# Four GNN layers on one core: norms scaled by ScalarE alone, part of VectorE's work given to GpSimd, kept blocks copied first, and a new order

## The chip, the cores and the metric

The kernel runs on one core of one Trainium2 chip. The metric is the device time of one execution, in microseconds (us). Every run below was in the fast state, and each was timed in turns with the kernel before on the same chip.

## The reference, cut to what matters

Sixteen graphs (batches) of 1024 nodes with 128 features go through four layers. All is fp32. Each layer adds its result to `x`.

```python
def layer(x, gnn):                       # 4 times
    h = jnp.maximum(_layernorm(x), 0.0)
    return x + gnn(h, adj, ...)

# layer 0, three times: a square of the nodes, weighted by the adjacency
h = h @ W + b
nh = h / jnp.maximum(jnp.linalg.norm(h, axis=-1, keepdims=True), EPS)
ew = adj * jnp.einsum('bij,bkj->bik', nh, nh)
h = jnp.einsum('bpq,bqc->bpc', ew, h)

# layer 1: (1 + eps) * x + adj^T x, then an MLP (128 -> 256 -> 128)

# layer 2: attention of tanh(s1 + s2); nodes without neighbours keep h ("lone nodes")
return jnp.where(su == 0, node_embedding, last_h)

# layer 3: gated attention over a symmetric square
att = jax.nn.softmax(jnp.where(adj > 0, e, 0), axis=1) * adj
h_prime = jax.nn.relu(jnp.einsum('bij,bjk->bik', att, h))
i_c, f_c, o_c = sigmoid(...), sigmoid(...), sigmoid(...)      # one per node
return o_c * jnp.tanh(jax.nn.sigmoid(i_c * h_prime + f_c * x))
```

## The kernel before

The kernel first writes down all its operations with an estimated duration, what they read and what they write. A planner then orders them in a simulated time: of the operations that an engine could begin now it takes the one with the smallest rank. The rank is the deadline of the batch, less the longest chain behind the operation, less a hand-set lead for its kind. The program is emitted in that order, so **each engine works through a fixed sequence**, and an operation whose input is late holds up all behind it on its engine.

```python
for o in reversed(self.ops):
    o.tail = o.us + max((s.tail + o.lat for s in o.succs), default=0.0)
    o.rank = (self.deadline(o.batch) - o.tail - self.leads.get(o.key, 0.0), o.seq)
```

Layer norms: VectorE scales four of the eight blocks, ScalarE the other four (and applies relu to its own; a separate ScalarE relu follows for VectorE's, except in layer 0):

```python
dve(1.03, [blk(xt, lo, hi), mv, rstd], [blk(hn, lo, hi)], lambda: scale_by_vector(*HALVES[0]), True)
lo, hi = HALVES[1]
act(1.55, [blk(xt, lo, hi), nb, rstd], [blk(hn, lo, hi)], lambda: scale_by_scalar(*HALVES[1]))
```

A symmetric square is computed by rows of blocks, half a row (512 columns, one PSUM bank) at a time. Blocks right of the diagonal are kept in SBUF (`above`), and the rows below turn them instead of computing them. A VectorE multiply reads each half row out of PSUM, and then ScalarE copies the kept blocks of the same bank:

```python
pc, view = square.row(j, s)                       # TensorE: matmul and turned blocks
dve(..., nc.vector.scalar_tensor_tensor(ew, view(), rn, adjT, op0=mult, op1=mult))
square.keep(j, s, pc)                             # ScalarE: copy of the kept blocks
```

Layer 3's rows, and its finish:

```python
# each row j: mask (VectorE), row maximum (VectorE), exp with sum (ScalarE), then
for lo, hi in HALVES:
    nc.vector.tensor_mul(span(e.t, lo, hi), span(e.t, lo, hi), span(aT[j].t, lo, hi))
# ... finish of a batch
nc.gpsimd.tensor_mul(z, hn, gate_f)               # GpSimd
add_scaled(z, D, 0, NB, hp, 0, E3, gate, 0, z, True)          # VectorE, 8 instructions
act(..., squash)                                  # two tanh
add_scaled(z, D, 0, NB, z, 0, D, gate, 2 * NB, xt, True)      # VectorE, 8 instructions
```

## Time and profile before

| | before |
|---|---|
| median (3 runs) | 2484.54 us (2484.53 to 2487.31) |
| span of the profiled run | 2481.8 us |
| what TensorE's rows need back to back (worked out in the prediction, which rounds it to 2371) | 2371.6 us |
| the rest | 110.2 us |

The rest can be placed in time. For a given TensorE row, sum the durations of all rows ahead of it in TensorE's order, and subtract the sum from the time at which the row really ran. I call the difference the **surplus**; what it grows by over a stretch is what TensorE lost there. I read it at each batch's first `psN` (the last projection of layer 3).

The waits of TensorE in the kernel before (columns: what waited for what, us in total, times, longest):

```profile
PE sq L619 <- ACT above L641: 27.8, 18, 2.0
PE ps_hT L451 <- DVE hn L553: 10.3, 1, 10.3
PE acc L671 <- DVE ew L791: 4.5, 3, 3.0
```

The first row is the copy of kept blocks, about once a batch; the second is the start of the program, which waits for the first norm.

### The profile page before, as it was taken

The numbers are of one execution on the slowest core, as the hardware profiler recorded it, in microseconds if no ns is written. First come the engines' busy times: TensorE is split into PE (matmuls) and PEld (weight loads), VectorE is DVE, ScalarE is ACT, GpSimd is POOL, SyncE is SP. The second block draws the span as 40 slices with busy tenths as digits, with TensorE's granted clock in tenths as the row PEclk, the third lists the DMA queues.
The fourth block names the chain that finished last, engine by engine and source line by source line (L and its number), as shares of the span: only waits on it lengthen the run. The fifth ranks groups of instructions, "written<-read, shape, count | busy, mean of one in ns | idle before, by whom it ended". The sixth has DMA issues, their size and how long they took to land.

```text
span 2481.8 us, 34726 instructions
## 1 busy us (share of the span) xinstructions
PE 2410.6 (97%) x11946; PEld 1588.7 (64%) x11946; DVE 2119.4 (85%) x5278; ACT 1287.1 (52%) x2401; POOL 214.4 (9%) x134
## 2 busy tenths in 40 slices
PE   6999999999999999999999999999999999999987
PEld 3567566675766657566675766756566575765763
DVE  6767989898897989889898897988989899796777
ACT  4425554644646455454554636456454655554575
POOL 1000010010101011011010100101011010010100
PEclk9999999999999999999999999999999999999998
DMA  7622827648284563936648276473945638054100
GB/s 125 129 67 69 163 59 143 138 80 167 60 160 121 99 140 84 165 91 127 129 94 178 52 154 135 84 154 68 165 107 111 136 85 162 1 108 80 35 1 18
DMA packets 1129441, 263.35 MB, mean 106 GB/s; under 512 B 971824, under 2 KB 1112880, under 8 KB 1129264
## 3 DMA queue, kind: packets, MB, share of 16 engines
q1 hardware_dynamic: 1108352, 251.73, 50.0%
q10 hardware_dynamic: 20912, 9.40, 1.4%
q8 instruction: 94, 1.54, 0.3%
q14 instruction: 83, 0.68, 0.1%
HBM read 198.14 MB, written 62.91 MB: 105 GB/s over the span
## 4 chain that ended last, share of the span: by engine, by line
PE 78%; DVE 9%; ACT 7%; issue 2%; DMA 1%; SPq 1%; ACTq 0%; POOL 0%; POOLq 0%; DVEq 0%
PE acc L671 31%; PE sq L609 17%; PE acc L682 11%; PE psP L461 6%; PE sq L619 4%; ACT e L906 3%; DVE ew L791 3%; ACT e L910 3%; PE py L844 2%; PE py L471 2%; DVE e L914 2%; PE ps_hTn L451 1%; DVE z L505 1%; PE pg L471 1%; PE ps_hnT L451 1%
## 5 line engine op out<-in xcount | busy, mean ns | idle before, releaser
L791 DVE SCALAR_TENSOR_TENSOR ew<-sq,rn,adjT 128x512 f32<-128x512 f32 x612 | 436.9, 739 | 68.2 <-PE sq L619 32.0
L671 PE MATMUL acc<-ew,h 128*128 128x512 f32 x1024 | 480.6, 597 | 4.7 <-DVE ew L791 4.5
L609 PE MATMUL sq<-hTn 128*128 128x512 f32 (+3 forms) x1152 | 441.3, 489 | 0.4 <-ACT hTn L483 0.4
L641 ACT COPY above<-sq 128x384 f32<-128x384 f32 (+3 forms) x432 | 169.2, 394 | 403.9 <-DVE ew L791 366.5
L671 PEld LDWEIGHTS acc<-ew,h 128*128 128x128 f32 x1024 | 178.9, 191 | 174.0 <-issue 112.9
L609 PEld LDWEIGHTS sq<-hTn 128*128 128x128 f32 x1152 | 193.5, 191 | 124.0 <-issue 76.1
L682 PEld LDWEIGHTS acc<-h,e 128*128 128x128 f32 x2048 | 241.0, 192 | 29.3 <-DVE e L914 11.8
L682 PEld LDWEIGHTS acc<-h,ew 128*128 128x128 f32 x2048 | 240.8, 192 | 21.0 <-DVE ew L791 11.4
L444 POOL TENSOR_TENSOR rstd<-ve,mhalf 128x8 f32<-128x8 f32 x64 | 104.8, 1637 | 1725.7 <-DVE ve L536 1694.9
L682 PE MATMUL acc<-h,ew 128*128 128x128 f32 x2048 | 252.7, 276 | 0.4 <-DVE ew L791 0.4
L682 PE MATMUL acc<-h,e 128*128 128x129 f32 x2048 | 249.5, 277 | 2.8 <-DVE e L914 1.5
L671 PE MATMUL acc<-e,hs 128*128 128x512 f32 x512 | 240.6, 595 | 1.7 <-DVE e L995 1.7
L671 PE MATMUL acc<-adjL,hn 128*128 128x512 f32 x512 | 239.0, 595 | 0.1
L988 ACT ACTIVATE e<-e,top 128x1024 f32<-128x1024 f32 x128 | 147.1, 1149 | 173.0 <-DVE top L984 172.5
L735 ACT ACTIVATE adjT<-adjT 128x1024 f32<-128x1024 f32 x128 | 135.0, 1055 | 194.0 <-DVE adjT L732 163.7
L619 PEld LDWEIGHTS sq<-ident,above 128*128 128x128 f32 x960 | 125.7, 141 | 142.2 <-issue 74.0
L619 PE MATMUL sq<-ident,above 128*128 128x128 f32 x960 | 174.4, 275 | 27.8 <-ACT above L641 27.8
L914 DVE SCALAR_TENSOR_TENSOR e<-adjT,e 128x512 f32<-128x512 f32 x256 | 162.0, 683 | 41.9 <-ACT e L910 41.9
L732 DVE STREAM_TRANSPOSE adjT<-adjT 128x1024 f32<-128x1024 f32 x128 | 155.2, 1225 | 17.8 <-DMA adjT<-in_adj_dram 10.9
L995 DVE TENSOR_TENSOR e<-e,adjT 128x512 f32<-128x512 f32 x256 | 166.2, 680 | 0.0
L906 ACT ACTIVATE e<-s,h 128x1024 f32<-128x1024 f32 x128 | 143.1, 1141 | 38.4 <-issue 36.6
L631 DVE STREAM_TRANSPOSE above<-sq 128x512 f32<-128x512 f32 x208 | 147.0, 707 | 10.5 <-PE sq L609 9.1
(124 smaller groups left out, 3455.9 us busy)
## 6 DMA issues: line engine op xcount, KB each, us to landing
adjT<-in_adj_dram SPq DMA_DIRECT2D x512, 128.0 KB, 3.7
adjL<-in_adj_dram SPq DMA_DIRECT2D x128, 512.0 KB, 4.9
by_hbm<-above SPq DMA_DIRECT2D x104, 512.0 KB, 3.2
got<-by_hbm SPq DMA_DIRECT2D x416, 128.0 KB, 3.0
x<-in_x_dram SPq DMA_DIRECT2D x16, 512.0 KB, 5.3
out_dram<-z ACTq DMA_DIRECT2D x16, 512.0 KB, 3.3
b<-in_L_gnn_b_dram ACTq DMA_DIRECT2D x4, 64.0 KB, 3.8
w<-in_L_gnn_W_dram ACTq DMA_DIRECT2D x2, 128.0 KB, 3.8
```

What stands on the lines that cost most here:

```text
L461: nc.tensor.matmul(dst.t[:, (c - lo) * n : (c - lo + 1) * n], cols(srcT.t, c), w, start=True, stop=True)
L609: lambda: nc.tensor.matmul(dst.t[:, (first - lo) * P :], cols(leftT.t, j), span(rightT.t, first, hi), start=True, stop=True),
L619: nc.tensor.transpose(cols(dst.t, r), cols(above.t, p), ident)
L641: lambda: nc.scalar.copy(span(above.t, p, p + hi - first), read.t[:, (first - lo) * P :]),
L671: lambda s=s, lo=lo, hi=hi: nc.tensor.matmul(acc[s].t, cols(h.t, at, w), span(ew.t, lo, hi), start=(j == 0), stop=(j == NB - 1)),
L682: nc.tensor.matmul(a.t[:, (c - lo) * n : (c - lo + 1) * n], cols(ew.t, c), h.t[:, j * w : j * w + n], start=(j == 0 and c == lo), stop=(j ...
L732: dve(V(N), [t], [t], lambda t=t: nc.vector.transpose(t.t, t.t), True)
L791: lambda view=view, ew=ew, rn=rn, j=j, lo=lo, hi=hi: nc.vector.scalar_tensor_tensor(by_block(span(ew.t, lo, hi), D, 4), view(), rn.t[:, j ...
L906: lambda e=e, j=j: nc.scalar.activation(e.t[:, 0:N], s1.t[:, 0:N], AF.Tanh, bias=h.t[:, j * E2 + D + 1 : j * E2 + D + 2]),
L914: lambda e=e, j=j, lo=lo, hi=hi: nc.vector.scalar_tensor_tensor(span(e.t, lo, hi), span(aT[j].t, lo, hi), 0.0, span(e.t, lo, hi), op0=ALU. ...
L988: lambda e=e, top=top, tot=tot: nc.scalar.activation(e.t[:, 0:N], e.t[:, 0:N], AF.Exp, bias=top.t, accum_out=tot.t),
L995: lambda e=e, j=j, lo=lo, hi=hi: nc.vector.tensor_mul(span(e.t, lo, hi), span(e.t, lo, hi), span(aT[j].t, lo, hi)),
```

## The change

The intent: VectorE is at 85%, and where it is late, TensorE stands. So take work off VectorE: norms wholly to ScalarE, layer 3's odd rows, layer 2's lone nodes and layer 3's two last scalings to GpSimd. Let the copy of kept blocks go ahead of VectorE's multiply of the same bank. Plan anew, with leads of their own for the first two and last two batches. The diff, cut to its core:

```diff
+            lead = self.leads.get(o.key + o.edge, self.leads.get(o.key, 0.0))
+            o.rank = (self.deadline(o.batch) - o.tail - lead, o.seq)
 ...
-    PERIOD, LAST, AHEAD, WINDOW = 66.0, 23.0, 2, 0.05
+    PERIOD, LAST, AHEAD, WINDOW = 83.0, 1.0, 2, 0.02
 ... (other buffer limits, all leads new; estimates +0.03 us on ScalarE, +0.015 on VectorE)
+    def on_pool(a, w, scalar, of_node, b, dst):
+        v = lambda: by_block(a.t, w)[:, :, 0:D]
+        pool_op(1.9, [a, scalar], [a], lambda: nc.gpsimd.tensor_mul(v(), v(), per_node(of_node())))
+        pool_op(1.9, [a, b], [dst], lambda: nc.gpsimd.tensor_add(by_block(dst.t), v(), by_block(b.t)))
 ... layer norm: both halves by ScalarE, with relu; no separate relu
+            for lo, hi in HALVES:
+                act(1.55, [blk(xt, lo, hi), nb, rstd], [blk(hn, lo, hi)], lambda lo=lo, hi=hi: scale_by_scalar(lo, hi))
 ... layers 0 and 3: the copy is declared ahead of the multiply
                     pc, view = square.row(j, s)
+                    if "k" in FLAGS:
+                        square.keep(j, s, pc)
                     o = dve(
 ...
-                    square.keep(j, s, pc)
 ... layer 2
-        add_scaled(xt, D, 0, NB, hn, 0, D, alone, 0, xt, True)
+            on_pool(hn, D, alone, lambda: alone.t, xt, xt)
 ... layer 3, rows 1, 3, 5, 7
+                pool_op(1.96, [e, aT[j]], [e], lambda e=e, j=j: nc.gpsimd.tensor_mul(e.t[:, 0:N], e.t[:, 0:N], aT[j].t))
 ... finish of layer 3 (the last batch in two halves): each of the two scalings
+                    pool_op(us, ..., lambda: nc.gpsimd.tensor_mul(part(a, w), part(a, w), per_node(of(g), n)))
+                    pool_op(us, ..., lambda: nc.gpsimd.tensor_add(part(z), part(a, w), part(c)))
 ... batch 0's input is loaded in two halves
```

## The prediction

> **What bounds the kernel now.** I read the page's first two parts, then the engine busy times over chosen stretches of time, then the waits and the timeline around the one wait that recurs, then the groups by form for the cost of what is moved.
>
> The page of the kernel before, busy time and forty slices:
>
> ```profile
> PE 2410.6 (97%) x11946; PEld 1588.7 (64%) x11946; DVE 2119.4 (85%) x5278; ACT 1287.1 (52%) x2401; POOL 214.4 (9%) x134
> ...
> PE   6999999999999999999999999999999999999987
> ...
> PEclk9999999999999999999999999999999999999998
> ```
>
> TensorE is full from the second slice to the last but one. So the question is how much of the span TensorE needs whatever the others do. The instruction orders of both kernels hold the same 3737 TensorE rows, differently ordered. From back-to-back pieces of the chain (a matmul stands there as two records): 512 columns take 0.859 us (8.59 us for 10, batch 0's layer 1), 128 columns 0.2234 (3.57 for 16, L844), 129 to 131 columns 0.227 (7.26 for 32, layer 2), a transpose 0.1097 (an estimate from the step between one and four in a row). 1504 x 0.859 + 128 x 0.644 + 128 x 0.43 + 1809 x 0.2234 + 1408 x 0.227 + 1988 x 0.1097 = **2371 us of TensorE demand**. The span is 2481.8, so all that any reordering can win is in the other **110 us**.
>
> Where these lie: I set the summed demand of all rows ahead of a batch's first psN (layer 3's last projection) against the time at which it runs. The surplus is 17.4 us at the first square (23.6 us), 31.8 at 80.5 us, 39.6 at batch 0's psN (307.7 us), then grows by 3.1 per batch to 74.6 at batch 11 (1959.9 us), is 78.2 at batch 13 (2274.9), 91.6 at batch 14 (2450.9), and 110 at the end. So **head 40, middle 35, tail 35**. Busy times over stretches (columns: stretch, its length, busy of TensorE, its weight loads, VectorE, ScalarE, GpSimd, then clock):
>
> ```profile
> 0.00:50.00 50.00, 32.77 (x124) 19.89 (x125) 28.06 (x74) 22.01 (x43) 7.29 (x10) 0.92 0.80 125
> 1209.86:1359.87 150.01, 148.22 (x735) 97.60 (x734) 133.64 (x333) 78.77 (x147) 13.35 (x9) 1.00 0.58 121
> 2125.10:2274.90 149.80, 149.62 (x759) 99.50 (x758) 121.51 (x291) 82.07 (x149) 11.72 (x7) 1.00 0.39 78
> 2274.90:2450.90 176.00, 168.47 (x915) 117.82 (x914) 139.88 (x373) 103.62 (x187) 13.36 (x8) 0.97 0.04 13
> 2450.90:2482.00 31.10, 13.07 (x60) 7.81 (x58) 19.07 (x54) 12.94 (x25) 3.79 (x2) 0.78 0.13 34
> ```
>
> The second row is one middle batch: demand 146.9 in 150.0 us, VectorE at 133.6 (89%). The third has VectorE at 121.5 (81%), and there demand (149.2) nearly fills the time: lighter VectorE, almost no loss. In the middle TensorE stands still only once a batch, and this is where:
>
> ```profile
> 1254.79 0.81 PE L609 MATMUL sq<-hTn 128*128 128x384 f32 x2
> ...
> 1255.99 0.74 DVE L791 SCALAR_TENSOR_TENSOR ew<-sq,rn,adjT 128x512 f32<-128x512 f32 x1
> ...
> 1256.77 0.48 ACT L641 COPY above<-sq 128x384 f32<-128x384 f32 x1 [6.14 <-DVE ew L791]
> ...
> 1257.30 0.33 PE L619 MATMUL sq<-ident,above 128*128 128x128 f32 x1 [1.70 <-ACT above L641]
> ```
>
> The square is finished at 1255.6, VectorE comes to it 0.4 us late, ScalarE (idle for 6.14 us) may copy the block only after that, and TensorE waits 1.70 us for the copy.
>
> **What the Trainium skill says.** "Perfetto Trace Analysis", Identifying the Most-Contended Engine: matmul busy time is a poor measure of the distance to the roofline, as matmuls are pipelined. The trace agrees: 2410.6 busy against 2371 of demand, so some 39 us of "busy" is stretched. "PSUM — Partial Sum Buffer", PSUM bank collisions raise a hardware error: two engines must not be in the same bank at once, so VectorE's multiply and ScalarE's copy of one square must follow each other; the trace shows the copies waiting for L791 for 366.5 us in 164 waits. "GPSIMD Engine Reference", Engine selection: elementwise work with two inputs is about twice as slow there as on VectorE. Here 1.90 us for 128x1024 against 2 x 0.68. "SBUF — State Buffer", Who interferes with whom: a VectorE instruction with two SBUF inputs and a GpSimd instruction that reads SBUF exclude each other. The kernel before has too little GpSimd work (9%) to show it.
>
> **The change part by part.** Costs by group and form (busy, mean ns of one; in a run of small ones they overlap):
>
> ```profile
> L995 DVE TENSOR_TENSOR e<-e,adjT 128x512 f32<-128x512 f32 x256 | 166.2, 680 | 0.0
> ...
> L560 ACT ACTIVATE hn<-x,nb,rstd 128x128 f32<-128x128 f32 x256 | 105.2, 484 | 26.1 <-DVE nb L544 25.0 <-DVE sum L1000 1.0
> ...
> L553 DVE TENSOR_SCALAR hn<-x,mv,rstd 128x128 f32<-128x128 f32 x256 | 70.4, 337 | 6.9 <-POOL rstd L444 6.9
> ...
> L505 DVE SCALAR_TENSOR_TENSOR x<-hn,alone,x 128x128 f32<-128x128 f32 x128 | 36.6, 357 | 1.3 <-ACT hn L575 1.3
> ...
> L1043 POOL TENSOR_TENSOR z<-hn,gate 128x1024 f32<-128x1024 f32 x16 | 30.4, 1897 | 73.0 <-PE sq L619 40.6 <-DVE gate L1038 21.4 <-PE p L895 11.0
> ```
>
> - Layer norms by ScalarE alone: VectorE loses 256 instructions, 70.4 us. ScalarE gains as many, +105.2, and loses 48 separate relus (30.4): +75.
> - Layer 3's odd rows on GpSimd: VectorE loses 128 of 256 L995, 83 us. GpSimd gains 64 x 1.9 = 122.
> - Layer 2's lone nodes and both last scalings on GpSimd: VectorE loses 3 x 128 small ones (36.6 + 34.5 + 34.5 = 106). GpSimd gains two instructions for each group, 6 per batch x 16 x 1.9 = 182.
> - Sum: VectorE 2119 - 259 = **1860 (75%)**, some 117 per middle batch; ScalarE about **1362 (55%)**; GpSimd about 214 + 304 = **518 (21%)**. No engine overtakes TensorE, and none of the 259 us is on its path: they only remove lateness.
> - Copy first: in the stop shown, the copy could begin at 1255.7 instead of 1256.77. With the lighter VectorE I expect the loss of 3.1 per middle batch to fall to about 1.5: 11.5 x 1.6 = **-18 us**.
> - Head: batch 0's input comes in halves, but its first norm is now ScalarE's alone, 8 x 0.41 = 3.3 us in place of 1.1 beside 1.6. These cancel. Loads of adj (all in the same order) set the rest. The own leads put batch 0 ahead of batch 1: **-4**.
> - Tail: in the new order all of batch 14 is done before batch 15's layer 3, whose last 31.6 us of demand now run alone; before, batch 14's last rows were mixed in. From its first transposes to the end the kernel before took 65.7 us (2416.1 to 2481.8). Now: some 9 us to the first square (12.7 before, 2416.1 to 2428.8, with 3.1 of batch 14's work between); VectorE's 8 rows, 16 x 0.66 + 8 x 1.21 + 8 x 0.65 + 8 x 0.15 = 26.7 (31.9 before), about 28 with waits; then from the last multiply to the end, 20.8 before. The finish goes from one pass of 8.9 us (1.9 + 2.2 + 2.2 + 2.2 and hops, below) to two halves with 10 GpSimd steps of about 1.05 in a row, 10.5 plus hops: +2. Sum about 59. Ahead of it, where 13 us were lost between batches 13 and 14, I expect 4 less.
>
> ```profile
> 2468.78 1.90 POOL L1043 TENSOR_TENSOR z<-hn,gate 128x1024 f32<-128x1024 f32 x1 [11.36 <-DVE gate L1038]
> 2470.71 2.19 DVE L505 SCALAR_TENSOR_TENSOR z<-hp,gate,z 128x128 f32<-128x128 f32 x8 [2.07 <-POOL z L1043]
> ...
> 2475.26 2.19 DVE L505 SCALAR_TENSOR_TENSOR z<-z,gate,x 128x128 f32<-128x128 f32 x8 [2.36 <-ACT z L1050]
> 2477.52 0.38 ACTq L1056 DMA_DIRECT2D out_dram<-z  x1
> ```
>
> Sum: at batch 15's first layer-3 transpose the demand done is 2340.0 in the new order. The surplus there was 87.1; less 18, 4 and 4 it is 61. 2340 + 61 + 59 = 2460 of span; timed runs lie 2.7 above the span (2484.5 against 2481.8): 2463. A steady loss nearer to the third stretch's 0.5 would give some 8 less. I choose **2460**.
>
> **The rivals.** (1) GpSimd excludes VectorE's two-input work: GpSimd reads SBUF for about 32 us of 147 per batch, VectorE's two-input work is about 40; chance overlap (an estimate) is 9 us per batch, under the 30 us that VectorE has free. But a row's chain gets longer, 1.3 to 1.9 us. If this costs what the relief brings: 2480. (2) Nearly every avoidable wait goes: middle loss 0.5, head and tail 10 less each: 2481.8 - 30 - 20 = 2432, timed 2434; just the 2% line. Needs all three. (3) The head is set by loads and the tail by its chain, so only the middle moves: 2466.
>
> **Range and chances.** Faster by over 2% means under 2434.9, so 50 of the 110 us, of which about 38 (first square at 17, end after the last multiply 21) are fixed. I give that 0.1. Slower by 2% would need a new bound; none is in sight: 0.01. Eight in ten: 2438 to 2476.
>
> **What would show it right or wrong.** TensorE busy near 2400 and 98%; VectorE near 1860; GpSimd near 520; the period of a middle batch 148.0 to 149; the 1.7 us wait for the copy gone or under 1; surplus at batch 0's psN about 35; the last transposes of layer 3 to the end about 59. It would be wrong if the middle period stayed at 150 (the lateness is not VectorE's), if VectorE's two-input groups rose well over 0.68 us (exclusion), or if head and tail gave far more than 8 us together.

## The result, and the profile after

The changed kernel took **2467.9 us** (median of 4, 2466.42 to 2469.86) against 2484.53 (2483.93 to 2487.31, 4 runs). The ratio is 0.9931, 95% interval 0.9914 to 0.9949: within 2%. Ratios here are the mean time of one kernel's fast runs over the mean of the other's fast runs of the same rounds, so not quite the ratio of the medians.

The page of the kernel after, busy time and two rows of the forty slices:

```profile
PE 2403.0 (97%) x11946; PEld 1595.3 (65%) x11946; DVE 1983.1 (80%) x4512; ACT 1357.6 (55%) x2612; POOL 576.5 (23%) x299
...
PE   7999999999999999999999999999999999999996
...
POOL 1001221311313122131311313122131311312125
```

TensorE is as full as before. ScalarE came out as forecast (1362), but VectorE is 123 us above the forecast of 1860, and GpSimd 58 above 518. Busy times over stretches (columns: stretch, length, busy of TensorE, weight loads, VectorE, ScalarE, GpSimd, clock, then DMA), the start and one middle batch:

```profile
0.00:50.00 50.00, 32.43 (x124) 19.16 (x125) 27.45 (x68) 24.20 (x51) 7.26 (x10) 0.96 0.82 131
1202.09:1350.38 148.29, 148.04 (x736) 97.80 (x735) 124.17 (x286) 83.28 (x160) 36.20 (x18) 1.00 0.64 121
```

A middle batch takes 148.3 us instead of 150.0. GpSimd's share went from 13 to 36 us. The waits of TensorE after:

```profile
PE acc L830 <- DVE ew L956: 12.1, 12, 1.1
PE ps_hT L566 <- ACT hn L702: 11.9, 1, 11.9
...
PE acc L819 <- DVE e L1198: 6.9, 6, 1.9
...
PE sq L767 <- ACT above L789: 2.2, 4, 1.1
```

The wait for the copy is nearly gone (27.8 to 2.2 us). In its place stands a wait for VectorE's multiply, eleven times about 1.07 us, in as many middle batches, and once 0.3. The timeline of the kernel after around one of them (columns: start, duration, engine, line, operation; in brackets the idle time before it and what ended it):

```profile
1734.23 2.43 POOL L1194 TENSOR_TENSOR e<-e,adjT 128x1024 f32<-128x1024 f32 x1 [5.95 <-ACT e L1189]
1734.37 2.84 DVE L1198 TENSOR_TENSOR e<-e,adjT 128x512 f32<-128x512 f32 x1
1734.46 0.37 ACT L789 COPY above<-sq 128x256 f32<-128x256 f32 x1 [0.30 <-PE sq L767]
...
1737.13 0.74 DVE L956 SCALAR_TENSOR_TENSOR ew<-sq,rn,adjT 128x512 f32<-128x512 f32 x1
...
1737.93 2.05 PE L830 MATMUL acc<-h,ew 128*128 128x128 f32 x16 [1.07 <-DVE ew L956]
```

GpSimd begins an odd row at 1734.23. VectorE begins half an even row 0.14 us later, and that 0.68 us instruction lasts 2.84: it ends at 1737.21, 0.55 us after GpSimd's. The multiply of layer 0 behind it belongs to the bank that the copy left at 1734.83; it begins only at 1737.13, and TensorE waits for it. (Rows 4, 5 and 6 keep three, two and one blocks, so the copy of 256 columns is row 5's, and the next one, of 128, is row 6's.) At 0.68 us VectorE's half row would have been over at 1735.05. The groups that show it in sum, of the kernel after:

```profile
L1194 POOL TENSOR_TENSOR e<-e,adjT 128x1024 f32<-128x1024 f32 x64 | 158.8, 2481 | 537.2 <-ACT e L1189 401.5 <-DMA got<-by_hbm 110.3 <-DMA by_hbm<-above 12.2
L1198 DVE TENSOR_TENSOR e<-e,adjT 128x512 f32<-128x512 f32 x128 | 119.4, 937 | 0.0
...
L943 DVE TENSOR_SCALAR ss<-ss 128x8 f32<-128x8 f32 x48 | 27.1, 565 | 1.5
L1054 DVE TENSOR_SCALAR hrow<-hsum 128x128 f32<-128x128 f32 x16 | 18.4, 1150 | 2.8 <-ACT hnT L619 2.8
```

The mean of VectorE's even rows rose from 680 to 937 ns. Two small ones rose more: `ss` to 565 ns and `hrow` to 1150, from 167 and 279 in the run b_drop below, which has before's program without the moved work. Sorted by whether a GpSimd instruction overlaps them: L1198 has 0.68 us alone and 1.26 on average (up to 2.85) beside L1194; `ss` has 0.17 alone and 1.75 beside the addition of the lone nodes. VectorE's instructions with an input in PSUM did not move (`ew<-sq` 0.74 alone, 0.74 beside L1252), nor did its row maxima (1.21 us, 1.21 in b_drop) and transposes of 1024 columns (1.24, 1.23 in b_drop). Where the VectorE instruction began first, it kept its time and GpSimd's grew (L1194: 2.59 us on average in these 30 cases, 2.39 in the other 34). This agrees with the Trainium skill, "SBUF — State Buffer", Who interferes with whom: only instructions with two inputs in SBUF, or in a two-port mode, contend, and the one that comes second waits. (Whether `ss` and `hrow` ran in such a mode no run shows.)

**Where the time went**, by surplus (us; the four parts and TensorE's 2371.6 add up to the span of the profiled run). The rows under "after" are the experiments of the next section:

| run | head: up to batch 0's psN | middle: batch 0 to 11 | batch 11 to 15 | finish | span |
|---|---|---|---|---|---|
| before | 39.6 | 35.0 | 18.9 | 16.7 | 2481.8 |
| after | 32.4 | 22.8 | 25.2 | 16.1 | 2468.1 |
| a_no5 | 34.4 | 26.0 | 28.6 | 15.6 | 2476.2 |
| a_noP | 32.9 | 37.9 | 27.3 | 12.0 | 2481.7 |
| a_noR | 36.4 | 46.0 | 32.1 | 16.1 | 2502.2 |
| a_fin | 33.6 | 20.6 | 23.5 | 11.9 | 2461.2 |
| a_noedge | 63.8 | 194.9 | 69.9 | 15.6 | 2715.8 |
| b_copy | 45.9 | 49.3 | 38.0 | 16.7 | 2521.5 |
| a_nocopy | 39.6 | 75.1 | 33.1 | 16.1 | 2535.5 |
| b_5P | 43.1 | 60.6 | 37.1 | 22.9 | 2535.3 |
| b_drop | 43.8 | 2.8 | 12.7 | 11.7 | 2442.6 |
| a_drop | 30.9 | 10.5 | 23.1 | 15.6 | 2451.7 |
| a_halves | 32.4 | 15.4 | 21.5 | 16.1 | 2457.0 |
| a_best | 33.1 | 12.8 | 21.9 | 12.3 | 2451.7 |

From before to after the head gave 7.2 and the middle 12.2. The two columns at the end must be read as a sum, as the order there is another: 35.6 before, 41.3 after. a_fin and a_best differ from after and a_halves only at the program's ends, yet their middles differ by 2.2 and 2.6: that is how far one profile can be trusted here.

### The profile page after: what moved, and what is told of

Its sections match the earlier page's. It is cut to its first block, busy times and chain, and to the rows that moved or that the text cites. A ratio compares the mean times of both kernels' runs of the same rounds, so it can differ in the third digit from the quotient of the medians.

```text
span 2468.1 us, 34654 instructions
## 1 busy us (share of the span) xinstructions
PE 2403.0 (97%) x11946; PEld 1595.3 (65%) x11946; DVE 1983.1 (80%) x4512; ACT 1357.6 (55%) x2612; POOL 576.5 (23%) x299
## 4 chain that ended last, share of the span: by engine, by line
PE 82%; DVE 8%; ACT 4%; DMA 3%; POOL 1%; issue 1%; SPq 1%; ACTq 0%; POOLq 0%; DVEq 0%
PE acc L819 32%; PE sq L757 17%; PE acc L830 15%; PE psP L597 4%; PE sq L767 3%; DVE ew L956 2%; PE py L1018 2%; PE py L607 2%; ACT hn L702 2%; PE ps_hTn L566 1%; DVE e L1198 1%; PE pg L607 1%; DMA got<-by_hbm 1%; PE ps_hnT L566 1%; DVE ss L943 1%
## 5 line engine op out<-in xcount | busy, mean ns | idle before, releaser
L757 PE MATMUL sq<-hTn 128*128 128x512 f32 (+3 forms) x1152 | 429.5, 487 | 0.4 <-ACT hTn L619 0.2
L1194 POOL TENSOR_TENSOR e<-e,adjT 128x1024 f32<-128x1024 f32 x64 | 158.8, 2481 | 537.2 <-ACT e L1189 401.5
L702 ACT ACTIVATE hn<-x,nb,rstd 128x128 f32<-128x128 f32 x512 | 205.8, 482 | 115.3 <-DVE nb L686 113.3
L1189 ACT ACTIVATE e<-e,top 128x1024 f32<-128x1024 f32 x128 | 146.9, 1148 | 103.0 <-DVE top L1185 101.9
L1106 DVE SCALAR_TENSOR_TENSOR e<-adjT,e 128x512 f32<-128x512 f32 x256 | 182.7, 767 | 10.4 <-ACT e L1102 10.4
```

The lines of the kernel that those rows point to most:

```text
L702: nc.scalar.activation(cols(hn.t, c), cols(xt.t, c), AF.Relu, bias=nb.t[:, c : c + 1], scale=rstd.t[:, c : c + 1])
L757: lambda: nc.tensor.matmul(dst.t[:, (first - lo) * P :], cols(leftT.t, j), span(rightT.t, first, hi), start=True, stop=True),
L1106: lambda e=e, j=j, lo=lo, hi=hi: nc.vector.scalar_tensor_tensor(span(e.t, lo, hi), span(aT[j].t, lo, hi), 0.0, span(e.t, lo, hi), op0=ALU. ...
L1189: lambda e=e, top=top, tot=tot: nc.scalar.activation(e.t[:, 0:N], e.t[:, 0:N], AF.Exp, bias=top.t, accum_out=tot.t),
L1194: pool_op(1.96, [e, aT[j]], [e], lambda e=e, j=j: nc.gpsimd.tensor_mul(e.t[:, 0:N], e.t[:, 0:N], aT[j].t))
```

## The experiments

**The theory** (LOCK, RELIEF): TensorE stands where VectorE is late; less work for VectorE is worth much, and GpSimd's long instructions give part of it back, because VectorE stands beside them. **Rivals**: the gain comes from the copies' new place (COPY), or from the new order alone (ORDER, MOVES), and VectorE's stretched instructions fall into its free time and cost nothing.

The kernels called a_ are the kernel after with its own emission order, those called b_ the kernel before with its own; what an operation emits, or its place, was edited. The ratios are to before's runs on the same chip. All results were right within the tolerance, but for those said to be wrong.

### First, each part undone in place: a_no5, a_noP, a_noR, a_fin

**a_no5**: the odd rows back on VectorE.

```diff
-   nc.gpsimd.tensor_mul(e.t[:, 0:N], e.t[:, 0:N], aT[j].t)
+   [nc.vector.tensor_mul(span(e.t, lo, hi), span(e.t, lo, hi), span(aT[j].t, lo, hi)) for lo, hi in HALVES]
```

> The changed kernel with its own order, but layer 3's odd rows are multiplied by VectorE again (two halves of 0.68 us), at the place in the order where GpSimd's instruction stood. Theory LOCK: in a middle batch the one wait of TensorE left (1.07 us, for layer 0's multiply) comes from GpSimd's 2.4 us multiply, which shuts out VectorE's two-input multiply (2.84 us instead of 0.68). Then that wait goes, the mean of L1198 falls from 937 ns to about 680, and the middle period stays near 148.5 or falls to about 147.5: 2455 to 2468 us. Theory RELIEF: VectorE's lower load made the gain. Then some 5 us per middle batch come back to VectorE, the period rises by 0.5 to 1.5 us: 2474 to 2485 us.

Measured: 2479.7 us (8 runs), ratio 0.9972 (0.9961 to 0.9982). The 1.07 us waits became 25 of 0.3 at most, but the middle got no shorter (26.0), so the time is 10 us above after by the ratios. The forecast of the theory LOCK was wrong and that of RELIEF held (2474 to 2485): giving the rows back takes the lock away and takes the relief away too. VectorE's busy time tells how much each is: 128 more instructions of 0.68 us are 87 us, but it rose by only 40.8 (to 2023.9). So 46 us of standing went.

**a_noP**: lone nodes and last scalings back on VectorE.

```diff
-   nc.gpsimd.tensor_mul(v(), v(), per_node(of_node())); nc.gpsimd.tensor_add(by_block(dst.t), v(), by_block(b.t))
+   for c in range(NB): nc.vector.scalar_tensor_tensor(cols(dst.t, c), cols(a.t, c, w), of_node()[:, c:c+1], cols(b.t, c), op0=ALU.mult, op1=ALU.add)
```

> The changed kernel with its own order, but layer 2's lone nodes and both last scalings are done by VectorE again (8 small instructions of about 0.27 us each, 2.2 us a group) in place of two GpSimd instructions of 1.9 and 2.35 us. Theory RELIEF: VectorE gets 6.6 us per middle batch back and the period rises by about 1: 2475 to 2485 us. Theory LOCK: six of GpSimd's instructions with SBUF reads go (about 12.5 us per batch), so VectorE's two-input work is shut out less; the gain balances the load: 2462 to 2470 us. In either case the finish of the last batch gets shorter, from 11.9 us between gate and store to about 6.5, worth 5 us of that.

Measured: 2483.06 us (12 runs), ratio 0.9987 (0.9978 to 0.9996); the middle lost 37.9. RELIEF was right: undone in after's order, this part costs 0.0056 of the 0.0069 that the change won by the ratios. Such shares don't add up (a_no5 costs 0.0041, and a_noR, the next run, 0.0130), so it isn't the part's share of the gain. VectorE took 106 us of work and rose by 39.0 (to 2022.1), so here 67 us of standing went. With a_no5's 46 that is 113 of the 123 us by which VectorE had missed its forecast.

**a_noR**: the first half of each norm back on VectorE, with its relu on ScalarE.

```diff
-   scale_by_scalar(lo, hi)
+   first_half() if lo == 0 else scale_by_scalar(lo, hi)     # scale_by_vector, then relu by ScalarE
```

> The changed kernel with its own order, but the first half of each layer norm is scaled by VectorE again (0.27 us for each of four blocks) and passed through a relu on ScalarE (0.62 us) in layers 1 to 3. VectorE gets 4.4 us per batch back, ScalarE loses 4.7. Theory RELIEF: 2470 to 2478 us. Rival: the norms sit between two layers and their latency falls by about 0.7 us each where a layer waits for them; no change or 2462 to 2468 us.

Measured: 2502.57 us, ratio 1.0061 (1.0044 to 1.0078). Both forecasts were too low. The wait that I had not reckoned with is ScalarE's for its relu behind VectorE's half (ScalarE's waits in a_noR):

```profile
ACT hn L709 <- DVE hn L695: 126.4, 44, 10.3
```

After's order has no room for that step, so this run tells what such a step costs in the wrong order, not what the part was worth in the change.

**a_fin**: only the last batch's two scalings back on VectorE.

```diff
+   back = b == B - 1     # VectorE's 8 instructions in place of GpSimd's pair
```

> The changed kernel, but the last batch alone is finished by VectorE (scale and add in one instruction, 4 blocks of 0.27 us for each half) in place of GpSimd's two instructions of 1.04 and 1.2 us. In the changed kernel the last gate is followed by ten GpSimd steps one after the other, 11.9 us to the last store. Theory: that chain is the end of the span and nothing else stands there, so it shrinks to about 6.5 us and the time by 4 to 6: 2462 to 2464 us. Rival: the store or ScalarE's tanh sets the end; under 2 us.

Measured: 2462.81 us, ratio 0.9906 (0.9891 to 0.9921), as expected. The finish fell from 16.1 to 11.9 us: where VectorE has nothing else to do, GpSimd's pair only lengthens the chain.

### Then the copy, the leads and the relief apart: b_copy, a_nocopy, a_noedge, b_5P

**b_copy**: before's order, each copy placed ahead of the multiply of its bank.

```diff
+   for tile_, copy in copies.items():
+       at, was = ordered.index(multiplies[tile_]), ordered.index(copy)
+       if was > at:
+           ordered.insert(at, ordered.pop(was))
```

> The kernel before in its own order, with one thing of the change: each of ScalarE's copies of kept blocks is emitted ahead of VectorE's multiplication of the same square. COPY (the middle's loss of 3.1 us per batch is half the 1.7 us wait of TensorE for such a copy in layer 1): that wait goes, the loss per batch falls to about 1.5, the middle from batch 0 to batch 11 loses 17 to 20 us instead of 35.0, and the time is 2466 to 2472 us (ratio 0.993 to 0.995). MOVES (the period is set by VectorE's whole load, and the wait is only where it shows): the 1.7 us appear as TensorE's wait for the multiplication or at another place, the middle stays above 31 us, and the time is 2480 to 2486 (ratio 0.998 to 1.000). Head and tail as before under both.

Measured: 2524.89 us, ratio 1.0148 (1.0133 to 1.0164). COPY was wrong, and MOVES too small: the middle lost 49.3. TensorE's wait for the copy fell to 2.5 us, and in its place VectorE waits (VectorE's waits in b_copy; before's list has no wait for a copy among those above 9 us):

```profile
DVE ew L796 <- ACT above L646: 95.9, 133, 2.2
...
DVE e L978 <- ACT above L646: 24.6, 30, 2.2
```

Copy and multiply of one bank follow each other in both kernels (before has the copy waiting for the multiply, 366.5 us in 164 waits). Here VectorE has to wait, and in this order that costs more.

**a_nocopy**: after's order, with 340 of 432 copies moved behind the multiply (the other 92 are needed earlier).

```diff
+       first = min(ordered.index(s) for s in copy.succs if s is not multiplies[tile_])
+       if was < at < first:
+           ordered.insert(at, ordered.pop(was))
```

> The kernel after in its own order, with 340 of its 432 copies moved back behind VectorE's multiplication of the same square (92 are needed earlier and stay). COPY: TensorE's waits for a copy (2.2 us in all in the profile of after, 27.8 in that of before) come back, at 0.7 to 1.7 us per batch, and the time is 2476 to 2492 us (ratio to before 0.997 to 1.003). MOVES: the middle keeps its 22.8 us within 4, and the time is 2465 to 2472 (ratio 0.992 to 0.995).

Measured: 2538.38 us, ratio 1.0203 (1.0186 to 1.022). COPY's direction was right, its size too small. TensorE's waits in a_nocopy:

```profile
PE sq L772 <- ACT above L794: 63.2, 52, 7.0
```

So each order is made for its place of the copies. The copies' place isn't a gain that can be added to another order.

**a_noedge**: after, planned again without the leads for the first two and last two batches.

```diff
-   lead = self.leads.get(o.key + o.edge, self.leads.get(o.key, 0.0))
+   lead = self.leads.get(o.key, 0.0)
```

> The kernel after, planned again without the own leads of the first two and the last two batches. EDGE (these leads made the head's 7.2 us and the last batches' overlap): the surplus at batch 0's last layer is 36 to 41 us instead of 32.4, what is lost from batch 13 to the end is 39 to 45 us instead of 36.6, and the time is 2472 to 2482 us. PLAN (the other leads, the period and the pools made them): head and tail stay within 2 us each, and the time is 2465 to 2471.

Measured: 2718.3 us, ratio 1.0929 (1.0913 to 1.0946). Neither theory. The whole order changed, not just its ends: from batch 7 to batch 11 each batch lost 13.5 us (surplus 204.9 to 258.7), against 2 in after, and the first four lost more. The leads are one set found together. What the edge leads alone are worth stays open.

**b_5P**: before's order, with the odd rows, lone nodes and last scalings on GpSimd.

```diff
+   if j % 2: nc.gpsimd.tensor_mul(e.t[:, 0:N], e.t[:, 0:N], aT[j].t)
-   add_scaled(xt, D, 0, NB, hn, 0, D, alone, 0, xt, True)      # and the two of z
+   by_pool(hn, D, alone.t, xt, xt)                             # mul and add, as in the change
```

> The kernel before in its own order, with the change's work for GpSimd alone: layer 3's odd rows, layer 2's lone nodes and layer 3's two last scalings; VectorE's norms, the copies and the order stay. RELIEF (VectorE's time off is worth something by itself): the middle's 35.0 us fall below 28 and the time is 2470 to 2480 us. ORDER (the relief is worth something only when the order is made for it, as the wait for a copy of 1.7 us per batch is not touched by it): the middle stays within 3 us of 35.0, and with GpSimd's longer operations in the last batch's finish, 2 to 5 us, the time is 2483 to 2494 us (ratio 0.999 to 1.004).

Measured: 2537.46 us, ratio 1.0201 (1.0186 to 1.0216). Worse than either theory had it: VectorE has 189 us less work, and the middle loses 60.6 us instead of 35.0. Either relief is worth nothing, or GpSimd takes back more than it gives. That was the question for the next runs.

The trace shows one way in which GpSimd takes back that neither theory had, and it isn't the lock. ScalarE issues the store of a finished batch (`ACTq` is its queue), and in this order the store stands ahead of exponentials of layer 2. It waits for the last scaling, now GpSimd's (the timeline of b_5P):

```profile
1256.27 2.36 POOL L520 TENSOR_TENSOR z<-z,x 128x1024 f32<-128x1024 f32 x1
...
1258.65 0.47 ACTq L1067 DMA_DIRECT2D out_dram<-z  x1
1259.17 2.19 ACT L913 ACTIVATE e<-s,h 128x1024 f32<-128x1024 f32 x2 [3.93 <-POOL z L520]
...
1262.33 1.29 DVE L921 SCALAR_TENSOR_TENSOR e<-adjT,e 128x512 f32<-128x512 f32 x2 [2.56 <-ACT e L917]
...
1263.08 8.26 PE L689 MATMUL acc<-h,e 128*128 128x129 f32 x68 [1.62 <-DVE e L921]
```

ScalarE stands for 3.93 us, VectorE behind it for 2.56, TensorE behind that for 1.62, in 12 batches. By an estimate, 11 x 1.63 = 18 of the 25.6 us that b_5P's middle loses beyond before's are this wait.

### Relief without GpSimd's load: b_drop, a_drop, a_halves

**b_drop**: b_5P without GpSimd's share; nobody does that work (wrong result on purpose). VectorE's program and the order are those of b_5P, but nothing waits for the missing work either.

```diff
-   nc.gpsimd.tensor_mul(e.t[:, 0:N], e.t[:, 0:N], aT[j].t)
+   pass                                                        # and the same for the other three
```

> The kernel before in its own order, without layer 3's odd rows on VectorE, without layer 2's lone nodes and without the two last scalings, and no other engine does them (wrong result on purpose). It is the run with before's order and GpSimd's load, but without that load: GpSimd's share in that run's 2537 us shows as the difference. RELIEF (VectorE's 189 us less are worth something by themselves): the middle loses 20 to 28 us instead of 35.0, the finish is some 4 us shorter, and the time is 2465 to 2478. ORDER (TensorE's waits are places in the order, not VectorE's load): the middle stays within 3 us of 35.0, and only the finish gets shorter: 2478 to 2483.

Measured: **2442.59 us**, ratio 0.9822 (0.9808 to 0.9837). The direction of RELIEF, and more than it had said: the middle loses 2.8 us instead of 35.0. One middle batch of b_drop, then of b_5P, same columns as above:

```profile
1196.32:1343.39 147.07, 147.07 (x735) 97.53 (x734) 123.57 (x301) 78.66 (x147) 13.36 (x9) 1.00 0.60 124
```

```profile
1226.94:1379.27 152.33, 148.62 (x735) 97.55 (x734) 130.90 (x301) 78.74 (x147) 35.92 (x19) 1.00 0.57 120
```

The two differ by GpSimd's 22.6 us, by VectorE's 7.3 us of longer instructions with the same 301 of them, and by 5.3 us of period. In b_drop TensorE is busy for all of 147.07 us, the demand of a middle batch (146.9 in the prediction). The groups of b_5P show the lock at work as in after, VectorE's even rows at 1110 ns; but the wait of ScalarE for GpSimd, shown above, is gone in b_drop too, so the two runs don't tell how much of the 57.8 us between their middles is the lock:

```profile
L1006 DVE TENSOR_TENSOR e<-e,adjT 128x512 f32<-128x512 f32 x128 | 139.6, 1110 | 0.0
```

And the wait for the copy fell to 8.7 us in b_drop with the copies where they were. It needed no new place for the copies.

What made VectorE late for that copy isn't settled by b_drop. In before the store waits as well, there for VectorE's eight small scalings (the timeline of before):

```profile
1237.94 2.14 DVE L505 SCALAR_TENSOR_TENSOR z<-z,gate,x 128x128 f32<-128x128 f32 x8
...
1240.16 0.38 ACTq L1056 DMA_DIRECT2D out_dram<-z  x1
1240.58 2.19 ACT L906 ACTIVATE e<-s,h 128x1024 f32<-128x1024 f32 x2 [3.03 <-issue]
```

ScalarE stands for 3.03 us, in 12 batches, and its exponentials are what VectorE works on next (it then waits 0.55 to 0.70 us for most of them). In b_drop the store has nothing to wait for, and that hold is gone. Laid beside before at the same row of TensorE (b_drop has it 13.57 us earlier), b_drop's exponentials begin 3.1 us earlier, and so does the multiply ahead of the copy (1239.32 + 13.57 against 1255.99). So b_drop takes away VectorE's work and ScalarE's hold together. 11 x 3.03 = 33 us of hold are as much as the 32.2 us that the middle won. The new order has the store later in ScalarE's sequence: after, a_no5, a_noP, a_nocopy, a_drop, a_halves and a_best show no such hold. What moving the store alone is worth in before's order was not tested.

**a_drop**: after, with the odd rows multiplied by nobody. (The result stays within the tolerance, but it is mathematically wrong: the adjacency's weights are missing from half of layer 3's rows.)

```diff
-   nc.gpsimd.tensor_mul(e.t[:, 0:N], e.t[:, 0:N], aT[j].t)
+   None
```

> The kernel after with layer 3's odd rows multiplied by the adjacency on no engine (wrong result on purpose; order and all else as after). LOCK (GpSimd's odd rows stretch VectorE's even rows to 937 ns and delay a multiply of layer 0 once per batch by 1.07 us, and this is why the middle saved 12.2 us and not 18): L1198's mean returns to about 690 ns, the recurring wait of 1.07 us goes, the middle from batch 0 to batch 11 loses 9 to 15 us instead of 22.8, and the time is 2452 to 2460 us. RHYTHM (what is left in the middle are places of the order, and exclusion falls into VectorE's free time): the middle stays at 19 to 24 us and the time is 2463 to 2468.

Measured: 2453.24 us, ratio 0.9863 (0.9848 to 0.9877); L1198's mean 693 ns; the 1.07 us waits gone; the middle 10.5 us. LOCK's forecast was right. In the new order, GpSimd's odd rows cost 12.3 us of the middle, as much as the whole change won there.

**a_halves**: after, each odd row in two instructions of 512 columns.

```diff
-   nc.gpsimd.tensor_mul(e.t[:, 0:N], e.t[:, 0:N], aT[j].t)
+   [nc.gpsimd.tensor_mul(span(e.t, lo, hi), span(e.t, lo, hi), span(aT[j].t, lo, hi)) for lo, hi in HALVES]
```

> The kernel after with each of GpSimd's odd-row instructions of 128x1024 cut into two of 128x512 (same work, same order, right result). LOCK, by length (VectorE stands for as long as one GpSimd instruction lasts, up to 2.84 us): the longest L1198 falls to about 1.9 us, the recurring 1.07 us wait falls under 0.4, the middle loses 14 to 19 us instead of 22.8, the time is 2459 to 2465. WORK (the exclusion goes by GpSimd's total time, however it is cut): L1198's mean stays near 900 ns, GpSimd's rows take 2 x 1.25 to 1.35 us, and the time is 2467 to 2474.

Measured: **2457.53 us**, ratio 0.9881 (0.9864 to 0.9897), a little better than LOCK had said. GpSimd works longer for the same rows (2 x 1.38 instead of 2.48 us), and TensorE loses 15.4 instead of 22.8 us in the middle. The mean of VectorE's even rows fell only to 864 ns, near the 900 that WORK had said, but the longest from 2.85 to 2.22 us. The same place as above in a_halves:

```profile
1727.85 3.03 POOL L1195 TENSOR_TENSOR e<-e,adjT 128x512 f32<-128x512 f32 x2 [5.79 <-ACT e L1189]
...
1727.99 1.76 DVE L1200 TENSOR_TENSOR e<-e,adjT 128x512 f32<-128x512 f32 x1
1728.08 0.37 ACT L789 COPY above<-sq 128x256 f32<-128x256 f32 x1 [0.30 <-PE sq L767]
...
1729.42 3.09 PE L830 MATMUL acc<-h,ew 128*128 128x128 f32 x24
...
1729.67 0.74 DVE L956 SCALAR_TENSOR_TENSOR ew<-sq,rn,adjT 128x512 f32<-128x512 f32 x1
```

VectorE gets in between the two halves after 1.76 us instead of 2.84. Row 5's multiply follows at 1729.67, 1.22 us after its copy and no longer 2.30, and TensorE's 24 matmuls run without a gap. The length of one GpSimd instruction counts for TensorE here, not GpSimd's total.

### A better version: a_best

After with three edits: odd rows in halves, the last batch's scalings on VectorE, and VectorE for the first half of the norm in the two places where it stands idle.

```diff
+   scale_by_scalar(lo, hi) if lo or k not in ("0_0", "15_3") else by_vector()     # and the edits of a_halves and a_fin
```

> The kernel after, in its own order, with three edits: layer 3's odd rows on GpSimd in halves of 512 columns (2457.5 us alone, where after has 2467.9); the last batch's two scalings back on VectorE (5.1 us less alone); and the first half of the norm on VectorE in batch 0's layer 0 and batch 15's layer 3 only, where VectorE stands idle. SUM (the three lie at different places, so their gains add): 2457.5 - 5.1 - 2 to 3 = 2449 to 2451 us, 2446 to 2454 with the scatter, ratio to before 0.983 to 0.987; TensorE's wait for the first hn falls from 11.6 to about 10 us and that for batch 15's hn from 2.1 to under 1. OVERLAP (head and tail are set by loads and by the chain of rows, so only the first two edits count): 2452 to 2456, waits as they were.

Measured: **2452.9 us**, ratio 0.9864 (0.9847 to 0.988), so 1.36% under before. It is the fastest kernel here whose result is fully right. The first two edits add up to it (2457.5 - 5.1 = 2452.4); the third gave nothing that shows. SUM's range with its scatter (2446 to 2454) holds the time as well as OVERLAP's does, so the waits decide: they did not shrink as SUM had said. TensorE's waits in a_best:

```profile
PE ps_hT L566 <- DVE hn L702: 12.1, 1, 12.1
...
PE ps_hnT L566 <- DVE gate L1286: 3.1, 1, 3.1
```

At the start VectorE was busy with batch 1's statistics when the first norm became ready. The first square still ran 1.3 us earlier (18.89 instead of 20.21 us), yet batch 0's surplus is 33.1 against 32.4: something behind it sets the head. At the end, the norm's work on VectorE delayed batch 14's gate.

## Why the prediction was right or wrong

The time was 2467.9, predicted 2460 with 2438 to 2476: inside, in the class that it gave 0.89. (Its sum gave 2460 of span and so 2463 of time; for choosing 2460 it has only a smaller middle loss that it thought possible, "some 8 less".) Of its own signs of being wrong, one came true: VectorE's two-input groups rose well over 0.68 us, the even rows to 937 ns. Its steps:

- **The frame was right.** TensorE's demand, not its busy time, is the floor (b_drop runs a middle batch in 147.07 us at a demand of 146.9); TensorE is busy for 2403.0 us (forecast near 2400), and no engine became a new bound.
- **The tail was right**: 59.9 us from batch 15's first layer-3 transpose (2408.18) to the end, forecast 59 (its own terms, 9 + 28 + 20.8 + 2, give 59.8). Its last step is half a microsecond longer than said (from the gate at 2452.84 to the last addition's end at 2464.3, 11.4 us, where 8.9 + 2 was said), and a_fin showed that the GpSimd pairs were the worse choice there by 4 to 5 us.
- **The surplus of 87.1 was read at the wrong row.** It belongs to before's first layer-3 transposes of batch 15, where the demand done is 2329, as some of batch 14's work came later there. At a demand of 2340.0, which the sum uses, before's surplus is 91.6. That is 4.5 us of the error.
- **The head** gave 7.2 instead of 4 (3.2 us the other way), the stretch from batch 13 to these transposes gave 5.0 instead of 4, and batches 11 to 13 lost 1.0 more than before, which the sum had left out.
- **The middle was mis-sized: "11.5 x 1.6 = -18 us" measured 12.2.** That is 5.8 us. Together: 4.5 + 5.8 - 3.2 - 1.0 + 1.0 = 7.1, against a surplus of 68.2 where the prediction had 61. That the head gave more than half of what the middle lacked is luck: no run shows why.

What kept the middle from more is shown for the odd rows. The step that failed is in the first rival: "chance overlap (an estimate) is 9 us per batch, under the 30 us that VectorE has free". The 9 was about right: VectorE's 123 us over its forecast are 7.7 per batch. The conclusion was wrong. Free time helps only if the delay falls into it; here VectorE stands for up to 2.85 us at a moment that the order fixes, with a multiply behind it for which TensorE waits. a_drop puts the odd rows' share in after's order at 12.3 us, and a_halves won 7.4 of these back by length alone. a_drop also takes GpSimd's 2.48 us out of each odd row's chain; how the 12.3 us divide between lock and chain is settled only as far as a_halves goes, but no wait of TensorE for GpSimd shows among after's. b_drop and b_5P lie 57.8 us apart in the middle, but there ScalarE's wait for GpSimd comes in as well, and I can't divide it.

The second failed step is the size of GpSimd's work: 1.9 us per instruction came from a row with a broadcast operand. With two full inputs it took 2.48 (odd rows), 2.35 (lone nodes' addition) and 2.18 to 2.39 (the scalings' additions). 64 x 0.58 + 16 x 0.45 + 15 x (0.28 + 0.49) = 56 us of the 58 that GpSimd ran over.

The reading of the 1.7 us wait was half right. VectorE was late, as said. That its load made it late isn't shown: in before its lateness follows ScalarE's 3.03 us behind the store, which the prediction overlooked, and b_drop ended both (27.8 to 8.7 us). That the copy's new place would end the wait was wrong as a reason: alone it costs 37 us (b_copy).

Where the prediction says that the trace agrees with "Perfetto Trace Analysis", it does so in that busy time is a poor measure. The page's reason is that pipelined instructions look smaller; here busy time, 2410.6 us, lies above the demand.

Open: how much of the middle's gain came from lighter VectorE and how much from the new order, the store's place in it above all. a_no5 and a_noP show that the relief is needed in the new order, not that it would have been enough in the old one. Open too: what made the head's 7.2 us. All a_ kernels that keep after's norms have about as much of it (30.9 to 34.4), but for a_nocopy (39.6) and a_noedge (63.8); the latter should have told, but broke the whole order.

## What to carry to other kernels

An engine's busy share says nothing about when it is late: b_drop and after both have VectorE at 124 us per middle batch, and one loses 0.3 us per batch and the other 2.1. If an engine is late, follow its wait back through every queue: here a store in ScalarE's sequence, waiting for another engine's last instruction, held exponentials that VectorE needed. Work moved to GpSimd was paid for here by those VectorE instructions that read SBUF twice, and by some small ones; first measure the move with the work simply left out, then cut GpSimd's instructions short, and give the work back where VectorE is idle. Leaving work out also takes away whatever waited for it, so read the waits of such a run before calling its gain relief. In a program whose order is planned for one set of durations, undoing a part in place measures the order as much as the part, so compare runs that share one order and one program on the engine in question.

## What the Trainium skill lacked or had wrong

- "GPSIMD Engine Reference", Engine selection, gives about 2x against VectorE for two inputs. Here, for 128x1024 fp32, it was 2.48 against 2 x 0.68 us (1.8x) with two full inputs, but 1.90 (1.4x) where one input is a per-node broadcast; the page has no figure for a broadcast operand.
- "SBUF — State Buffer", Who interferes with whom, has the rule right, but not what it costs in a pipelined kernel: 1.75 us for a 0.17 us `tensor_scalar` of 128x8, 2.84 for a 0.68 us `tensor_tensor`, and at most 0.7% of before's time for the odd rows (a_drop against after by their ratios). It also doesn't say that cutting GpSimd's instruction in two helps (0.5% of the time, a_halves against after by their ratios), though GpSimd then works 0.28 us longer per row.
- No page says how large the effect is when operations only change places: b_copy and a_nocopy moved copies within an order, a_noedge was ordered anew, and they cost 37, 68 and 248 us against the kernel that they were made from (by the ratios).
